# Causal convolution with per-position tap weights: where the tap weights of the fourth tap group are kept, and which engine multiplies with them

## The chip, the cores and the metric

The kernel runs on one core of a Trainium2 chip. The metric is the device time of one execution in microseconds; the time before is the median of three runs, 1239.92 us (1238.9 to 1240.16). The profile is that of one further execution.

The engines that are named here: PE is the matrix engine (TensorE), DVE the vector engine (VectorE), ACT the activation engine (ScalarE), POOL is GpSimd, and SP (SyncE) issues transfers. SBUF is the large on-chip memory, PSUM the small one into which PE writes. [...]

## The reference, cut to what matters

The network has four parts, each added to the residual: a causal convolution, a feed-forward layer with 4-bit rounding, a layer with a learned update, and a mixture of experts. The change lies in the first part alone:

```
avg  = cumsum(x, axis=1) / arange(1, l + 1)          # running mean, per channel
ci   = avg, split into H = 16 heads of d = 8 channels
pc   = ci @ W_pe + b_pe                              # 2 * 31 values per head and position
energy = stt + sigmoid(gate) * dyn                   # 31 energies
w    = softmax(energy, axis=-1)                      # 31 tap weights per head and position
out  = sum over k of w[:, :, k] * padded[:, k : k + l, :]   # for each of the 8 channels
v    = out @ W_fc.T + residual; then a layernorm
```

There are B = 8 sequences of L = 512 positions with 128 channels.

## The kernel before

`sequence_conv` works through the eight sequences. The 31 taps are cut into four groups g = 0 to 3 of eight taps, so that 16 heads x 8 taps fill the 128 partitions, and a row holds the 512 positions. For a sequence b and a group g:

- `gate` and `tap` (matmuls at L358, two banks of the pool `ps_e` in turn) give the two halves of `pc`. ACT turns the gate into a sigmoid in two steps (L366, L367). `energy` on DVE forms the energy `en` (L390) and the running maximum `top` (L394, L396).
- `turn_top` (PE, L401), `greatest` (DVE L406, then an ACT copy `mw`, L408) and `turn_greatest` (PE `mb`, L413) bring the largest energy of each head and position back to all partitions. `less` (DVE, L416) subtracts it from all four groups at once.
- `weigh` (ACT) takes the exponential twice: for groups 0 to 2 into a PSUM tile `w` (L427), each group with a bank of its own (tags w0, w1, w2 of the pool `ps_w`), and for all four groups into SBUF, in place (`en`, L429).
- `part_sums` and `sums` (PE `pn` L435, ACT copy `dn` L440, PE `sm` L445) add up the weights; `invert` (DVE L449, ACT L451) and `turn_inverse` (PE `rb` L456, ACT copy `rbs` L458) spread the inverse over the partitions. The tiles tt, mb, pn, sm and rb all use the single bank of the pool `ps_m`, so each waits until the one before it has been read. `mb` therefore waits for the copy `rbs`.
- The products of weights and shifted inputs. `base` holds, for the eight channels of a head, the shifted inputs; it comes by way of DRAM (`far` L349, eight loads L352, issued by SP). For groups 0 to 2 DVE multiplies six channels (`product`, L484, 128x3072, weights from PSUM), POOL two (`shared`, L473, two instructions of 128x512, weights from SBUF). For group 3 DVE multiplies all eight channels, with weights from SBUF (128x4096), in the sequences 0 to 5. In the sequences 6 and 7 `last_weights` (ACT, L463) copies the weights of group 3 into a bank of `ps_e`, and POOL takes two channels there too.
- `add_up` (PE `cv`, L493, 16 matmuls) sums a group's products over taps into one bank. The product tiles `pr` have three buffers in turn. `scale_down` (DVE, L500), `project` (PE, L505, L506), `norm1` (DVE statistics, then small POOL steps) and `finish` (ACT L524, POOL L528, L529) end a sequence; `means` (PE `av` L343, ACT copy `avg` L346) begins one.

The sequences are interleaved by hand: in the loop over b, `cur` is being multiplied while the energies of `nxt` and the gates of `then` are formed, and the end of `old` is worked off. On PE, DVE, ACT and in most of POOL's work the order of instructions is the order in which the program calls them: `Line` ties each instruction to the one before it on its engine. What an engine waits for, everything behind it on that engine waits for too.

In the loop the part that matters reads, before the change, in this order: `product(cur, 1)`, `greatest(nxt)`, `turn_inverse(cur)`, `taps(then, 0)`, `turn_greatest(nxt)`, `add_beta(b)`, `add_up(cur, 1)`, `norm1(old)`, `scaled(b + 4)`, then (sequences 6 and 7 only) `last_weights` and `shared` of group 3, `product(cur, 2)`, `add_up(cur, 2)`, and towards the end `less(nxt)`, `weigh(nxt, 0, 1)`, `means(b + 3)`, `weigh(nxt, 1, 4)`, `product(cur, 3)`, `add_up(cur, 3)`. Sequence 0 is written out ahead of the loop in much the same order.

Of the kernel before, what the change touches and what calls it, by code (L numbers as in the profile page):

```python
# [8 lines left out]
F32 = mybir.dt.float32  # L9
# [5 lines left out]
PSUM = bass.MemoryType.PSUM  # L15
DRAM = bass.MemoryType.DRAM

P = 128
B, L, D = 8, 512, 128
# [111 lines left out]
def flat(ap):  # L131
    return ap.rearrange("p a b -> p (a b)")
# [17 lines left out]
def sequence_conv(cx):  # L150
# [11 lines left out]
    nc, tc, ins = cx.nc, cx.tc, cx.ins  # L162
    KK, NGR = 8, 4
    NJ, ND = 4, 2
    NV, NP = 6, 3
# [6 lines left out]
    with ExitStack() as st:  # L172
# [4 lines left out]
        ps_e = st.enter_context(tc.tile_pool(name="a_pse", bufs=2, space=PSUM))  # L177
        ps_m = st.enter_context(tc.tile_pool(name="a_psm", bufs=1, space=PSUM))
        ps_c = st.enter_context(tc.tile_pool(name="a_psc", bufs=1, space=PSUM))
        ps_p = st.enter_context(tc.tile_pool(name="a_psp", bufs=1, space=PSUM))  # L180
        ps_w = st.enter_context(tc.tile_pool(name="a_psw", bufs=1, space=PSUM))
        vec, ten, act, gp = cx.vec, cx.ten, cx.act, cx.gp


# [83 lines left out]
        def stats0(lo, hi):  # L268
            for b in range(lo, hi):
                stats(grp(cx.x, b), mv0[:, b * G : (b + 1) * G, :])  # L270
# [90 lines left out]
        def gate(s, g, place=(ps_e, "e")):  # L361

            e = spread(s, 1, g, "eg", place)
            sg = p2.tile([P, L], F32, tag="sg", name="sg", bufs=4)
            s.setdefault("sg", {})[g] = sg
            act(nc.scalar.activation(sg, e, AF.Tanh, bias=half[:, g : g + 1], scale=0.5))  # L366
            act(nc.scalar.activation(sg, sg, AF.Copy, bias=0.5, scale=0.5))  # L367

        def tap(s, g):

            s.setdefault("ev", {})[g] = spread(s, 0, g, "ev")
# [5 lines left out]
        def taps(s, half_):  # L377
            for g in (2 * half_, 2 * half_ + 1):
                tap(s, g)
# [5 lines left out]
        def energy(s, g):  # L385
            if g == 0:
                s["en"] = p2.tile([P, NGR, L], F32, tag="en", name="en", bufs=3)
                s["top"] = p2.tile([P, L], F32, tag="top", name="top")
            en, top = s["en"], s["top"]
            vec(nc.vector.scalar_tensor_tensor(  # L390
                en[:, g, :], s["ev"][g], bias[:, 0, g : g + 1], s["sg"][g], ALU.add, ALU.mult
            ))
            if g == 0:
                vec(nc.vector.tensor_scalar(top, en[:, 0, :], bias[:, 2, 0:1], None, ALU.add))  # L394
            else:
                vec(nc.vector.scalar_tensor_tensor(top, en[:, g, :], bias[:, 2, g : g + 1], top, ALU.add, ALU.max))  # L396
# [6 lines left out]
        def greatest(s):  # L403

            mx = p2.tile([P, G, H], F32, tag="mx", name="mx")
            vec(nc.vector.tensor_reduce(mx, s["tt"].rearrange("p j (h k) -> p j h k", h=H), AX.X, ALU.max))  # L406
            s["mw"] = mw = p2.tile([P, G, H, KK], F32, tag="wide", name="mw")
            act(nc.scalar.copy(mw, mx.unsqueeze(3).to_broadcast([P, G, H, KK])))  # L408
# [12 lines left out]
        def weigh(s, lo, hi):  # L421

            en = s["en"]
            for g in range(lo, hi):
                if g < NP:
                    w = ps_w.tile([P, L], F32, tag=f"w{g}", name="w")
                    act(nc.scalar.activation(w, en[:, g, :], AF.Exp, bias=bias[:, 2, g : g + 1]))  # L427
                    s["w"].append(w)
                act(nc.scalar.activation(en[:, g, :], en[:, g, :], AF.Exp, bias=bias[:, 2, g : g + 1]))  # L429
# [12 lines left out]
        def sums(s):  # L442
            s["sm"] = sm = ps_m.tile([P, G, H], F32, tag="m", name="sm")
            for j in range(G):
                ten(nc.tensor.matmul(sm[:, j, :], s["dn"][:, j * P : (j + 1) * P], fold, start=True, stop=True))  # L445
# [7 lines left out]
        def turn_inverse(s):  # L453
            rb = ps_m.tile([P, G, P], F32, tag="m", name="rb")
            for j in range(G):
                ten(nc.tensor.transpose(rb[:, j, :], s["rw"][:, j].rearrange("p a b -> p (a b)"), cx.ident))  # L456
            s["rbs"] = rbs = p2.tile([P, L], F32, tag="rbs", name="rbs")
            act(nc.scalar.copy(rbs, flat(rb)))  # L458

        def last_weights(s):  # L460

            w = ps_e.tile([P, L], F32, tag="e", name="w")
            act(nc.scalar.copy(w, s["en"][:, NP, :]))  # L463
            s["w"].append(w)

        def shared(s, lo=0, hi=NP):

            s.setdefault("pr", [])
            for g in range(lo, hi):
                pr = p2.tile([P, DH, L], F32, tag="pr", name="pr", bufs=3)  # L470
                for d in range(NV, DH):
                    at = slice(KK * g, KK * g + L)
                    gp(nc.gpsimd.tensor_tensor(pr[:, d, :], s["base"][:, d, at], s["en"][:, g, :], ALU.mult))  # L473
                s["pr"].append(pr)

        def product(s, g, lo=0, hi=DH):

            if g == len(s["pr"]):
                s["pr"].append(p2.tile([P, DH, L], F32, tag="pr", name="pr", bufs=3))
            in_psum = g < len(s["w"])  # L480
            hi = min(hi, NV if in_psum else DH)
            w = s["w"][g].unsqueeze(1) if in_psum else s["en"][:, g : g + 1, :]
            at = slice(KK * g, KK * g + L)
            vec(nc.vector.tensor_tensor(  # L484
                s["pr"][g][:, lo:hi, :], s["base"][:, lo:hi, at], w.to_broadcast([P, hi - lo, L]), ALU.mult
            ))
# [11 lines left out]
        def scale_down(s):  # L498
            s["cs"] = cs = p2.tile([P, L], F32, tag="cs", name="cs", bufs=1)
            vec(nc.vector.tensor_tensor(cs, s["cv"], s["rbs"], ALU.mult))  # L500
# [39 lines left out]
        vec(nc.vector.tensor_scalar(half, bias[:, 1, :], 0.5, None, ALU.mult))  # L540
        stats0(3, 5)
        cur = seq[0]
        for g, place in enumerate(((ps_w, "w0"), (ps_w, "w1"), (ps_w, "w2"), (ps_c, "c"))):
            gate(cur, g, place)
            tap(cur, g)
            energy(cur, g)
# [33 lines left out]
        gates(then, 0)  # L580
        stats0(5, B)
        greatest(nxt)
        turn_inverse(cur)
        taps(then, 0)
        turn_greatest(nxt)
# [18 lines left out]
        for b in range(1, B):  # L604
            cur, nxt, then, old = seq[b], seq.get(b + 1), seq.get(b + 2), seq.get(b - 1)
            shared(cur)
            product(cur, 0)
            if b > 1:
                finish(seq[b - 2], nc.gpsimd)
            part_sums(cur)  # L610
            sums(cur)
            if old:
                scale_down(old)
                project(old)
            add_up(cur, 0)
            if nxt:
                for g in (2, 3):
                    energy(nxt, g)
            invert(cur)
            if nxt:  # L620
                turn_top(nxt)
            if then:
                gates(then, 0)
            product(cur, 1)
            if nxt:
                greatest(nxt)
            turn_inverse(cur)
            if then:
                taps(then, 0)
            if nxt:  # L630
                turn_greatest(nxt)
            add_beta(b)
            add_up(cur, 1)
            if old:
                norm1(old, nc.gpsimd)
            if b + 4 < B:
                scaled(b + 4)
            if b == B - 3:
                ffn.load(flat(tri)[:, : ffn.NW], cur["spread"])
            if b >= B - 2:  # L640
                last_weights(cur)
                shared(cur, NP, NGR)
            product(cur, 2)
            add_up(cur, 2)
            if then:
                for g in (0, 1):
                    energy(then, g)
                gates(then, 1)
                taps(then, 1)
            if nxt:  # L650
                less(nxt)
                weigh(nxt, 0, 1)
            if b + 3 < B:
                seq[b + 3] = means(b + 3)
            if nxt:
                weigh(nxt, 1, NGR)
            if b < B - 1:
                product(cur, 3)
                add_up(cur, 3)
# [9 lines left out]
        q = Fp4.of(cx, ffn.raw, ffn.NW, inv[:, :nb], inv[:, P : P + nb], parts, quot)  # L669
# [7 lines left out]
        q.scales()  # L677
        q.divide()
        act(nc.scalar.activation(warm, cx.eps[1e-5], AF.Silu))
        q.addends([ps_w.tile([P, L], F32, tag=f"w{i}", name="up")[:, : hi - lo] for i, (lo, hi) in enumerate(q.parts)])  # L680
        pj, v = cur["pj"], p2.tile([P, G, D], F32, tag="v", name="v")
        mv = p2.tile([P, G, 2], F32, tag="mv", name="mv")
        for _ in norm.stats(1):
# [21 lines left out]
        place = p2.tile([P, L], F32, tag="sg", name="quot", bufs=4)  # L705
# [1369 lines left out]
```

## Time and profile before

| what | value |
|---|---|
| median of three runs | 1239.92 us |
| the profiled execution | 1229.96 us |
| its span, first to last instruction | 1228.1 us |
| granted TensorE clock, mean | 0.976 |
| busy share of the span: PE, DVE, ACT, POOL | 91%, 62%, 41%, 60% |
| PE weight loads, beside the matmuls | 56% |
| start of `sm` (L445) of the sequences 1 to 7 | 73.03, 99.41, 125.75, 152.09, 178.43, 202.79, 224.49 us |

The shares of the whole span mix parts that have different limits. The convolution takes about the first 240 us. Since each sequence has its `sm` matmuls once, the distances between their starts are the time per sequence: 26.38, 26.34, 26.34, 26.34, 24.36 and 21.70 us.

A timeline row gives start, duration, engine, line, operation, output and inputs with their shapes; in brackets stands how long the engine was idle before it, and what ended that. A row of the chain of waits gives start, duration, engine and tile.

### The profile page before, as it was taken

The numbers are of one execution on the slowest core, as the hardware profiler recorded it, in microseconds if no ns is written. First come the engines' busy times: TensorE is split into PE (matmuls) and PEld (weight loads), VectorE is DVE, ScalarE is ACT, GpSimd is POOL, SyncE is SP. The second block draws the span as 40 slices with busy tenths as digits, with TensorE's granted clock in tenths as the row PEclk, the third lists the DMA queues.
The fourth block names the chain that finished last, engine by engine and source line by source line (L and its number), as shares of the span: only waits on it lengthen the run. The fifth ranks groups of instructions, "written<-read, shape, count | busy, mean of one in ns | idle before, by whom it ended". The sixth has DMA issues, their size and how long they took to land.

```text
span 1228.1 us, 15912 instructions
## 1 busy us (share of the span) xinstructions
PE 1112.0 (91%) x5475; PEld 682.0 (56%) x5475; DVE 761.9 (62%) x1801; ACT 498.8 (41%) x1050; POOL 736.0 (60%) x728
## 2 busy tenths in 40 slices
PE   7999998767987999999988999999999997999993
PEld 4333343345666555555566555555476666878773
DVE  6899999989996544444455444444466887123364
ACT  4655544445667322222244222223343444243331
POOL 1356666745644888888822888888500666355563
PEclk8999999989999999999999999999999998999997
DMA  5223444951000000000000000000000111221256
GB/s 157 90 82 94 120 117 141 383 150 49 1 1 1 1 1 1 1 1 1 0 1 1 1 1 1 1 0 1 1 1 3 43 44 43 63 70 53 67 199 208
DMA packets 54607, 67.29 MB, mean 55 GB/s; under 512 B 6927, under 2 KB 32350, under 8 KB 54528
## 3 DMA queue, kind: packets, MB, share of 16 engines
q1 hardware_dynamic: 48544, 56.57, 15.2%
q0 software_dynamic: 4608, 8.43, 2.1%
q10 hardware_dynamic: 1376, 1.29, 0.3%
q8 instruction: 43, 0.70, 0.2%
q14 instruction: 36, 0.29, 0.1%
HBM read 40.00 MB, written 27.13 MB: 55 GB/s over the span
## 4 chain that ended last, share of the span: by engine, by line
PE 63%; DVE 19%; ACT 9%; issue 4%; POOL 2%; DMA 2%; ACTq 0%; DVEq 0%; POOLq 0%
PE ph L1614 5%; PE sum L1589 5%; PE pp L1604 5%; PE sum L1588 4%; PE po L1998 4%; PE sum L1590 4%; PE pb L1566 4%; PE pa L1564 4%; PE ph L1985 4%; DVE v L859 3%; PE cv L493 2%; DVE pr L484 2%; PE pt L1597 2%; PE o L1354 2%; PE gu L974 2%
## 5 line engine op out<-in xcount | busy, mean ns | idle before, releaser
L1577 POOL TENSOR_TENSOR ds<-sw,s 128x512 f32<-128x512 f32 x64 | 81.2, 1268 | 74.9 <-DVE sw L1572 74.9
L1579 POOL TENSOR_TENSOR ds<-ds,s 128x512 f32<-128x512 f32 x64 | 110.4, 1725 | 5.0
L1570 ACT COPY b<-pb 128x512 f32<-128x512 f32 x64 | 37.5, 586 | 169.6 <-PE pb L1566 164.6
L1811 POOL DMA_INDIRECT rows<-xr,slot x64 | 62.6, 978 | 66.2 <-PE ph L1338 30.9
L1988 ACT ACTIVATE ht<-ph,b 128x512 f32<-128x512 f32 (+2 forms) x104 | 57.0, 576 | 107.3 <-PE ph L1985 105.9
L473 POOL TENSOR_TENSOR pr<-base,en 128x512 f32<-128x512 f32 x52 | 75.0, 1472 | 38.0 <-ACT en L429 37.3
L2012 POOL DMA_INDIRECT res<-ye,xe x60 | 58.5, 974 | 64.4 <-DVE ye L2010 28.0
L1574 DVE TENSOR_TENSOR h<-sw,b 128x512 f32<-128x512 f32 x64 | 50.0, 781 | 75.6 <-ACT b L1570 75.5
L484 DVE TENSOR_TENSOR pr<-base,w 128x3072 f32<-128x3072 f32 (+2 forms) x27 | 86.3, 3206 | 0.8 <-ACT w L427 0.8
L1578 POOL TENSOR_TENSOR ds<-sw,ds 128x512 f32<-128x512 f32 x64 | 82.8, 1294 | 5.0
L1580 POOL TENSOR_TENSOR ds<-ds,b 128x512 f32<-128x512 f32 x64 | 81.9, 1280 | 5.0
L1604 PEld LDWEIGHTS pp<-proj,ht 128*128 128x128 f32 x512 | 67.1, 191 | 30.8 <-issue 29.7
L1599 ACT COPY ht<-pt 128x512 f32<-128x512 f32 x64 | 37.6, 587 | 103.0 <-PE pt L1597 103.0
L1998 PE MATMUL po<-w,ht 128*128 128x128 f32 (+1 forms) x640 | 77.1, 277 | 0.0
L1985 PE MATMUL ph<-xt,w 128*128 128x512 f32 (+2 forms) x208 | 72.3, 492 | 3.9 <-DVE xt L1968 3.9
L1572 DVE TENSOR_TENSOR sw<-pa,s 128x512 f32<-128x512 f32 x64 | 44.3, 692 | 49.4 <-ACT s L1568 49.4
L1998 PEld LDWEIGHTS po<-w,ht 128*128 128x128 f32 (+1 forms) x640 | 73.9, 188 | 0.6
L1616 DVE TENSOR_TENSOR db<-ph,sw 128x512 f32<-128x512 f32 x64 | 44.3, 692 | 45.3 <-PE ph L1614 45.3
L1614 PE MATMUL ph<-proj_t,dpt 128*128 128x512 f32 x128 | 71.6, 641 | 0.0
L493 PE MATMUL cv<-pr,sel 128*32 128x512 f32 x512 | 61.4, 605 | 8.9 <-DVE pr L484 8.8
L1564 PE MATMUL pa<-gate,kt 128*128 128x512 f32 x128 | 66.0, 598 | 3.0 <-ACT qt L1197 0.9
L1604 PE MATMUL pp<-proj,ht 128*128 128x128 f32 x512 | 67.5, 275 | 0.0
(366 smaller groups left out, 2604.5 us busy)
## 6 DMA issues: line engine op xcount, KB each, us to landing
base<-far SPq DMA_DIRECT2D x64, 268.0 KB, 5.5
rows<-empty SPq DMA_DIRECT2D x1, 5005.0 KB
res<-zero SPq DMA_DIRECT2D x1, 4096.0 KB, 26.8
own<-zero SPq DMA_DIRECT2D x2, 2048.0 KB, 18.8
w<-in_L_ffn_W SPq DMA_DIRECT2D x16, 256.0 KB, 5.0
y<-res SPq DMA_DIRECT2D x16, 256.0 KB, 5.3
xe<-rows SPq DMA_DIRECT2D x7, 585.0 KB, 4.3
y<-own SPq DMA_DIRECT2D x12, 256.0 KB, 4.7
```

The costliest lines, as they stand in the source:

```text
L473: gp(nc.gpsimd.tensor_tensor(pr[:, d, :], s["base"][:, d, at], s["en"][:, g, :], ALU.mult))
L484: vec(nc.vector.tensor_tensor(s["pr"][g][:, lo:hi, :], s["base"][:, lo:hi, at], w.to_broadcast([P, hi - lo, L]), ALU.mult))
L493: ten(nc.tensor.matmul(s["cv"][32 * j : 32 * (j + 1), :], sel[:, i].rearrange("p a h -> p (a h)"), s["pr"][g][:, i * NJ + j, :], start=(g ...
L1564: nc.tensor.matmul(pa, ki, gate, start=True, stop=True)
L1577: nc.gpsimd.tensor_tensor(ds, sw, s, ALU.mult)
L1578: nc.gpsimd.tensor_tensor(ds, sw, ds, ALU.subtract)
L1579: nc.gpsimd.tensor_tensor(ds, ds, s, ALU.add)
L1580: last = nc.gpsimd.tensor_tensor(ds, ds, b, ALU.mult)
L1604: nc.tensor.matmul(pp, ht[:, c * P : (c + 1) * P], proj[:, c, :], start=(c == 0), stop=(c == NF - 1))
L1614: nc.tensor.matmul(ph, dpt, proj_t, start=True, stop=True)
L1985: ten(nc.tensor.matmul(ph[:, :n], self.w1[:, e, c * P : (c + 1) * P], xt[:, :n], start=True, stop=True))
L1998: ten(nc.tensor.matmul(po[:m, i - lo, :], ht[:, c, (i - lo) * P : (i - lo) * P + m], self.w2[:, e, c, :], start=(c == 0), stop=(c == NF - ...
```

## The change

The pool `ps_w` has one tag with three banks that are taken in turn, where each group had a bank of its own. The weights of group 3 are copied into one of these banks (`last_weights`) in every sequence, and POOL multiplies two channels of group 3 in every sequence, DVE the other six. `last_weights` now stands between `greatest(nxt)` and `turn_inverse(cur)`. Each sequence takes four tiles from three banks: the tile of group 2 of the next sequence gets the bank in which the group 3 weights of this sequence were.

```diff
-        ps_w = st.enter_context(tc.tile_pool(name="a_psw", bufs=1, space=PSUM))
+        ps_w = st.enter_context(tc.tile_pool(name="a_psw", bufs=3, space=PSUM))
...
                 if g < NP:
-                    w = ps_w.tile([P, L], F32, tag=f"w{g}", name="w")
+                    w = ps_w.tile([P, L], F32, tag="w", name="w")
                     act(nc.scalar.activation(w, en[:, g, :], AF.Exp, bias=bias[:, 2, g : g + 1]))
...
         def last_weights(s):
 
-            w = ps_e.tile([P, L], F32, tag="e", name="w")
+            w = ps_w.tile([P, L], F32, tag="w", name="w")
             act(nc.scalar.copy(w, s["en"][:, NP, :]))
             s["w"].append(w)
...
-        for g, place in enumerate(((ps_w, "w0"), (ps_w, "w1"), (ps_w, "w2"), (ps_c, "c"))):
+        for g, place in enumerate(((ps_w, "w"), (ps_w, "w"), (ps_w, "w"), (ps_c, "c"))):
...
         greatest(nxt)
+        last_weights(cur)
+        shared(cur, NP, NGR)
         turn_inverse(cur)
...
             if nxt:
                 greatest(nxt)
+            last_weights(cur)
             turn_inverse(cur)
...
-            if b >= B - 2:
-                last_weights(cur)
-                shared(cur, NP, NGR)
+            shared(cur, NP, NGR)
             product(cur, 2)
...
-        q.addends([ps_w.tile([P, L], F32, tag=f"w{i}", name="up")[:, : hi - lo] for i, (lo, hi) in enumerate(q.parts)])
+        q.addends([ps_w.tile([P, L], F32, tag="w", name="up")[:, : hi - lo] for i, (lo, hi) in enumerate(q.parts)])
```

## The prediction

> **What bounds the kernel now.** The change lies in the first 240 us, so I read that stretch alone. First the busy time of each engine in one sequence, from one `sm` to the next (columns: PE, PE weight loads, DVE, ACT, POOL, then clock, DMA share, GB/s):
>
> ```profile
> core 0: us, PE busy (x) PEld busy (x) DVE busy (x) ACT busy (x) POOL busy (x), PEclk, DMA share, GB/s
> 125.75:152.09 26.34, 24.59 (x133) 10.49 (x133) 25.49 (x25) 15.20 (x28) 16.03 (x27) 1.00 0.33 94
> ```
>
> DVE is busiest (25.49 of 26.34 us), but PE is only 0.9 us behind it. Shares can't say which of the two sets the 26.34. So next the waits of both engines in three such sequences (99.41 to 178.43 us; total, times, longest):
>
> ```profile
> PE sm L445 <- ACT dn L440: 3.3, 4, 0.8
> PE mb L413 <- ACT rbs L458: 1.6, 3, 0.5
> PE pn L435 <- ACT en L429: 0.9, 3, 0.3
> ...
> DVE mx L406 <- PE tt L401: 1.7, 3, 0.6
> DVE rs L449 <- PE sm L445: 0.3, 2, 0.2
> ```
>
> DVE waits for PE, twice a sequence; PE waits for ACT and never for DVE. So PE and ACT turn in a ring, each waiting for the other, and DVE follows it. The chain of waits says the same:
>
> ```profile
> 125.75 1.07 PE sm L445 x8
> ...
> 133.99 0.63 ACT sg L367
> 134.62 0.51 ACT mw L408
> 135.67 0.66 PE mb L413 x4
> 136.32 3.57 PE cv L493 x32
> 139.89 1.07 PE eg L358 x2
> ...
> 144.09 2.17 PE av L343 x8
> 146.29 0.59 ACT avg L346
> ...
> 152.09 1.06 PE sm L445 x8
> ```
>
> It goes from PE to ACT at the gates (132.03), back to PE at `mb`, to ACT at the second gates and at `avg`, back to PE at `sm`, and round again after exactly 26.34 us. No DVE row is in it from 99.41 to 183.23. The timeline of ACT shows the place that matters:
>
> ```profile
> 134.53 0.60 ACT L408 COPY mw<-mx 128x512 f32<-128x512 f32 x1
> 135.03 0.58 ACT L458 COPY rbs<-rb 128x512 f32<-128x512 f32 x1
> 135.51 1.65 ACT L301 ACTIVATE xn<-x,off,rs 128x128 f32<-128x128 f32 x4
> ```
>
> ACT works without a gap from 132.03 to `rbs`, which ends at 135.61; `mb` starts on PE at 135.67, after an idle 0.53 us that the PE timeline puts down to `rbs`. Whatever is put ahead of `rbs` on ACT is on the ring.
>
> Where the ring is not the bound, at the first and the sixth sequence, PE waits for the very product that the change makes shorter:
>
> ```profile
> 68.61 1.92 PE L493 MATMUL cv<-pr,sel 128*32 128x512 f32 x16 [1.33 <-DVE pr L484]
> ...
> 198.07 1.92 PE L493 MATMUL cv<-pr,sel 128*32 128x512 f32 x16 [1.30 <-DVE pr L484]
> ```
>
> **Removed on DVE.** Six products of 128x4096 become 128x3072. Neighbours in the DVE timeline: the large one starts at 140.92, the next (3072, weights in PSUM) at 145.26, the one after at 148.52. So 4.34 against 3.26 us: 1.08 us each, 6.5 us in all. In the ring sequences (1 to 4) none of it shows: DVE only waits longer for PE.
>
> **Added on POOL.** Twelve 128x512 products. Such pairs took 2.53 to 2.75 us, so 2.7 a sequence. POOL comes free at 131.65 (`add_beta`), then waits 1.38 for the statistics; the pair would end at about 134.4 and push the 18 small steps of `norm1` from ending at 138.01 to about 140.8. Behind them: ACT's `v` (L524, 150.07), 9 us cover, and POOL's next products, which wait for `en` until 145.0, 4 us cover. The pair needs the buffer that `cv` of group 0 read until 130.54: no wait. `cv` of group 3 needs the pair at 146.18. So 0; without cover up to 2.7 a sequence.
>
> [...]
>
> **Added on ACT, the term that decides.** Six copies `w` of 128x512 from SBUF to PSUM. In the sequences 6 and 7 the same copy (L463, 210.69 and 230.40) took 0.60 and 0.59. What it takes of ACT's queue is the distance to the next start: between like copies 0.50 (`mw` to `rbs`) and 0.48 (`rbs` to `xn`). Bounds: 0.48, and the full 0.60. I take 0.50, the row at the same place. It stands right ahead of `rbs`, so `rbs`, `mb` and everything after move by 0.50 in each sequence.
>
> - Sequence 0: `mb` 56.71 to 57.21. Down PE: `av` ends at 67.79 for 67.29, the shorter product ends at about 67.4 for 68.56, so `cv` starts at 67.8 for 68.61. But `pn` also needs ACT's exponentials, behind `avg`, which follows `av`: the third ended at 70.60 and will at 71.1; in the steady sequences `pn` ends 1.72 after it (149.55 to 151.27), so at 72.8, where it ended at 72.36. The 0.8 that DVE gives is lost, and `sm` comes 0.46 late.
> - Sequences 1 to 4: 0.50 each on the ring, 2.00.
> - Sequence 5: no `means` is left, the chain before passes to DVE (from 183.85 to 222.4 without a gap). `sm` of 6 is 0.50 later still (2.96), but DVE has gained 1.08 and loses about 0.6, since product 0 of sequence 6 now waits for its weights from ACT (`w` at 196.16, which moves to 199.1). `tt` of the last sequence then ends at 208.19 + 2.96 = 211.15 and DVE's `mx` starts there, for 208.73 before: 2.42. DVE's own path would have it at about 210.9. So this sequence adds nothing (2.46 to 2.42).
> - Sequences 6 and 7 had the copy already, behind `rbs`. Now it delays `mb` at 210.85 by about 0.3; `less` follows product 2, which ends at 213.71, 2.2 after `mb`: covered. In 7 ACT is idle 3.11 us before `rbs`: covered.
>
> **Banks in turn.** The `w` of group 2 waits until DVE has read the group 3 weights of the sequence before. Behind it on ACT: two more `en`, `v`, `dn`, that is the ring. DVE's product ends near 144.2, `w` comes at 148.13 + 0.5: 4 us cover. In the last sequence it is `w` at 218.63 against a product end at 219.19, 0.6 late; the last `en` ends at 221.2 for 220.7, and `pn` starts at 221.82 after its own wait for `cv`. So 0; with the cover gone a microsecond late is one on the ring. The two `ps_e` banks that this frees in 6 and 7 save nothing: no gates are left to wait for them.
>
> **SP.** The eight loads of `base` for sequence 2 now stand ahead of `far` of sequence 3 (6.23 us of issue at 68.64). That `far` is next needed at 94.69, 19 us later. The weight `w_down` of the next layer moves behind loads too; its tile is first read at 236.92, 60 us on. So 0, and a late `base` would cost its lateness.
>
> **Sum.** 0.46 + 2.00 - 0.04 = +2.4 us on the profiled execution: 1229.96 to 1232.4. The timed runs are 10 us longer than it (1239.92), and no page says where. If PE is the slower part there, the ring also binds in sequence 5, and its 0.50 counts: +2.9. I take the middle, +2.7: 1242.6. With 0.60 a copy and six of them: +3.6, 1243.5. Own range of this case: 1241.8 to 1243.6. After the convolution all is in series with it, and moves as a whole.
>
> **The rivals.**
> - DVE is the bound after all (for: 25.49 of 26.34 busy; in the second sequence 26.20 of 26.38; against: it waits for PE, PE never for it). Then 6 x 1.08 = 6.5 us come out: 1233.4. This is the other side; it decides if DVE is later than PE at `cv` of group 3, where it was 0.84 us early (145.34 against 146.18). Chance 0.10.
> - The copy costs nothing, because ACT finds room ahead of `rbs` (against: no gap from 132.03 on). Then only the end counts: DVE would be 1.08 early at `mx`, of which `tt` leaves 208.73 - 208.19 = 0.5. So 1239.4. Chance 0.13.
> - The turn of the banks or POOL's added work gets onto the ring. POOL's lock also lengthens DVE's `top` (L396 1.46 beside POOL, 0.75 alone). If `w` of group 2 is held 1 us in six sequences: 1242.6 + 6 = 1248.6. Against: 4 us cover. Chance 0.09.
> - That the change doesn't do what it says is ruled out by its instruction order: all eight sequences have the 128x3072 product, the POOL pair and the copy ahead of `rbs`.
>
> **How the numbers follow.** The forecast has 0.68. Runs of this kernel can tell about 0.2% from no change, 2.5 us, so the line lies at 1242.4, inside the forecast's own range. Of 0.68, 0.43 lie above it and 0.25 below; with the bank rival slower is 0.52. Same is 0.25 and the free copy's 0.11: 0.36. Faster is the DVE rival and the rest of the free copy: 0.12. The range takes in the free copy at nearly its full price and reaches past six copies of 0.60 towards the bank rival: 1239.0 to 1245.0.
>
> **What would show it.** Right: the distance from `sm` to `sm` is 26.84 for 26.34; PE's idle time before `mb` is 1.0 for 0.53; on ACT the row L463 stands between L408 and L458; DVE waits for PE about 1 us more a sequence, most of it ahead of `mx`, `cs` or the first product; the products of 128x4096 are gone; POOL's L473 has 64 rows. Wrong: a distance below 26.34, which says that DVE was the bound, or `w` of group 2 with an idle time ended by DVE.

## The result and the profile after

The kernel after the change takes 1244.2 us (median of 20 runs, 1241.87 to 1248.39), the kernel before 1240.41 us (20 runs beside them). The ratio is 1.0031, with an interval of 1.0021 to 1.0040: 3.8 us slower, between 2.6 and 5.0. The forecast was 1242.6 us, 2.7 us more than before.

The profiled executions can't be subtracted from each other: the one after has a span of 1240.2 us, 12.1 more than the 1228.1 before. Where these 12.1 us lie follows from the start times of the same instructions in the two traces:

| stretch | before, us | after, us | difference |
| --- | --- | --- | --- |
| start to `sm` of sequence 0 | 42.23 | 39.61 | -2.6 |
| `sm` of 0 to `sm` of 6 | 160.56 | 163.62 | +3.06 |
| `sm` of 6 to `sm` of 7 | 21.70 | 20.16 | -1.5 |
| on to the last pass of the learned layer (first `ph`, L1338 before, L1339 after) | 699.3 | 700.9 | +1.6 |
| that pass, to the first expert's `ph` (L1985 before, L1986 after) | 131.2 | 141.6 | +10.4 |
| the rest of the span | 173.1 | 174.3 | +1.2 |

Only the second row is shown by the experiments to be the change. A second profile of the kernel before (b_again) differs from the first by 2.5 us in the first row alone, the clock differs in the third (0.92 before, 1.00 after), and the 10.4 us come with the chip, as b_again shows (131.1 us in that pass on its chip, 142.3 in e1_copy_behind_rbs on another). In the steady sequences it is the same each time: from `sm` to `sm` the six distances were 30.80, 26.38, 26.34, 26.34, 26.34 and 24.36 us, and are 31.31, 26.89, 26.85, 26.85, 26.85 and 24.87. Every one is 0.51 longer. First the engines' busy times in one steady sequence after (columns as in the prediction):

```profile
124.66:151.51 26.85, 24.58 (x132) 10.50 (x133) 24.90 (x25) 15.70 (x29) 18.55 (x29) 1.00 0.33 96
```

DVE has lost 0.6 us of work (25.49 to 24.90) and POOL has gained 2.5 (16.03 to 18.55); PE does the same work as before (24.59 and 24.58), and the sequence is longer than it was. DVE's product alone became 1.08 shorter; part of that is gone again because `top` (L396) beside POOL's products took 1.74 us here where it took 1.46. ACT's timeline in the same sequence, and PE's `mb` after and then before:

```profile
133.44 0.60 ACT L408 COPY mw<-mx 128x512 f32<-128x512 f32 x1
133.95 0.58 ACT L463 COPY w<-en 128x512 f32<-128x512 f32 x1
134.47 0.58 ACT L458 COPY rbs<-rb 128x512 f32<-128x512 f32 x1
134.94 1.65 ACT L301 ACTIVATE xn<-x,off,rs 128x128 f32<-128x128 f32 x4
```

```profile
135.10 0.66 PE L413 MATMUL mb<-ident,mw 128*128 128x128 f32 x4 [1.05 <-ACT rbs L458]
```

```profile
135.67 0.66 PE L413 MATMUL mb<-ident,mw 128*128 128x128 f32 x4 [0.53 <-ACT rbs L458]
```

The new copy L463 stands between `mw` and `rbs`. From its start to the next one are 0.52 us, where its duration reads 0.58: like copies overlap by 0.06. `mb` starts 0.63 after `rbs` begins (0.64 before), and PE's idle time ahead of it has grown from 0.53 to 1.05. The waits of three such sequences (97.81 to 178.36 us; total, times, longest) answer to those of the prediction:

```profile
PE sm L445 <- ACT dn L440: 3.3, 4, 0.8
PE mb L413 <- ACT rbs L458: 3.1, 3, 1.0
PE pn L435 <- ACT en L429: 0.9, 3, 0.3
DVE cs L500 <- PE cv L493: 2.0, 3, 0.7
DVE mx L406 <- PE tt L401: 1.7, 3, 0.6
DVE pr L484 <- ACT w L427: 1.3, 3, 0.4
DVE rs L449 <- PE sm L445: 0.2, 1, 0.2
```

One wait has changed on PE, the one for `rbs` (1.6 to 3.1). PE still waits for nothing of DVE. DVE now waits in two new places, ahead of `cs` (0.7 each) and of the first product (0.4 each): together 1.1 a sequence, which is the 0.6 us of work that it lost and the 0.5 by which the sequence became longer. No DVE row stands in the chain of waits from 97.81 to 182 us. And the two places at which PE had waited 1.33 and 1.30 us for the long product are gone; the row of sequence 0 now has no idle time in front of it:

```profile
65.11 1.92 PE L493 MATMUL cv<-pr,sel 128*32 128x512 f32 x16
```

Even so sequence 0 became 0.51 longer: the start of `cv` isn't what its `sm` waits for. PE waits behind that `cv` for ACT's exponentials (0.29 us) and `dn` (0.68 us).

### The profile page after: what moved, and what is told of

It is laid out like the page before. It is cut to its first block, busy times and chain, and to the rows that moved or that the text cites. A ratio compares the mean times of both kernels' runs of the same rounds, so it can differ in the third digit from the quotient of the medians.

```text
span 1240.2 us, 15948 instructions
## 1 busy us (share of the span) xinstructions
PE 1109.6 (89%) x5475; PEld 678.0 (55%) x5475; DVE 759.1 (61%) x1801; ACT 502.3 (41%) x1056; POOL 747.1 (60%) x740
## 4 chain that ended last, share of the span: by engine, by line
PE 65%; DVE 17%; ACT 11%; issue 4%; DMA 2%; POOL 2%; ACTq 0%; DVEq 0%; POOLq 0%
PE ph L1615 5%; PE sum L1590 5%; PE pp L1605 5%; PE sum L1589 4%; PE sum L1591 4%; PE po L1999 4%; PE pb L1567 4%; PE pa L1565 4%; PE ph L1986 4%; PE cv L493 3%; DVE v L860 3%; PE pt L1598 2%; PE o L1355 2%; PE ph L1339 2%; ACT sg L366 2%
## 5 line engine op out<-in xcount | busy, mean ns | idle before, releaser
L473 POOL TENSOR_TENSOR pr<-base,en 128x512 f32<-128x512 f32 x64 | 85.9, 1371 | 40.8 <-ACT en L429 34.4
L484 DVE TENSOR_TENSOR pr<-base,w 128x3072 f32<-128x3072 f32 (+2 forms) x33 | 106.4, 3233 | 2.9 <-ACT w L427 2.9
L1986 PE MATMUL ph<-xt,w 128*128 128x512 f32 (+2 forms) x208 | 70.9, 484 | 4.0 <-DVE xt L1969 3.9
L1590 PE MATMUL sum<-db,k 128*128 128x512 f32 x128 | 66.1, 598 | 1.6 <-DVE db L1617 1.6
```

The lines of the kernel that those rows point to most:

```text
L484: vec(nc.vector.tensor_tensor(s["pr"][g][:, lo:hi, :], s["base"][:, lo:hi, at], w.to_broadcast([P, hi - lo, L]), ALU.mult))
L1590: nc.tensor.matmul(sums[1], ki, db, **kw)
L1986: ten(nc.tensor.matmul(ph[:, :n], self.w1[:, e, c * P : (c + 1) * P], xt[:, :n], start=True, stop=True))
```

## Experiments

All ratios are to the kernel before, run on the same chip beside the experiment, with 95% intervals.

The first four kernels, on one chip (before: 1241.3 us), take the change apart. The diffs are cut to the lines that matter: sequence 0, written out ahead of the loop, is edited in the same way. Theory: the place of the one ACT copy is the whole cost. Rivals: POOL's extra pairs, the turn of the three banks (each holds one 128x512 tile of the pool `ps_w`) or products of DVE and POOL that hold each other up cost something, or the shorter product gives something back.

**e1_copy_behind_rbs.** The changed kernel, with the copy behind `rbs`. POOL pairs, short products and banks in turn stay.

```diff
             if nxt:
                 greatest(nxt)
-            last_weights(cur)
             turn_inverse(cur)
...
             if b + 4 < B:
                 scaled(b + 4)
+            last_weights(cur)
```

> The changed kernel with one thing moved: ACT copies the group 3 weights behind rbs and the scaling, not ahead of rbs; POOL's pairs, DVE's smaller products and the banks in turn stay. Theory 'ring' (the copy ahead of rbs lengthens the PE-ACT ring, nothing else costs): sm to sm in the steady sequences back from 26.85 to 26.34 us, PE's idle time before mb back from 1.05 to 0.53, time 0 to 1 us below the kernel before (ratio 0.999 to 1.000). Rival 'POOL and banks' (POOL's added products, their lock against DVE, or the wait for a bank cost the time): sm to sm stays near 26.85 and the ratio near 1.003.

Measured 1241.31 us, 0.9999 [0.9990, 1.0008]. PE and ACT in the steady sequence:

```profile
135.76 0.66 PE L413 MATMUL mb<-ident,mw 128*128 128x128 f32 x4 [0.53 <-ACT rbs L458]
```

```profile
137.16 0.57 ACT L463 COPY w<-en 128x512 f32<-128x512 f32 x1
```

PE's wait is back at 0.53, `sm` to `sm` at 26.34. The copy is still made, in time that ACT had free: behind it ACT is idle for another 3.35 us until the next gates. Everything else in the change together costs nothing that can be seen, and gives nothing.

**e2_copy_alone.** The changed kernel, with the copy where it was put but without its use in sequences 0 to 5: DVE multiplies all eight channels of group 3 again, and POOL's pair is gone.

```diff
             last_weights(cur)
+            if b < B - 2:
+                cur["w"].pop()
             turn_inverse(cur)
...
-            shared(cur, NP, NGR)
+            if b >= B - 2:
+                shared(cur, NP, NGR)
```

> The changed kernel with the copy and the banks in turn, but in sequences 0 to 5 nobody uses the copied weights: DVE multiplies all eight channels of group 3 from SBUF as before, POOL takes none. Ring: sm to sm 26.85, idle before mb 1.05, ratio 1.003 to 1.004. POOL and banks, if POOL is the cost: sm to sm 26.34, ratio 1.000; if the banks are: sm to sm near 26.85, but with an idle time before the w of group 2 that DVE ends.

Measured 1244.62 us, 1.0028 [1.0018, 1.0037]. `sm` to `sm` is 26.85 and the wait ahead of `mb` 1.05, as with the whole change. So the copy costs the same whether DVE's product is shorter or not.

**e3_copy_twice.** The changed kernel, with the copy made twice.

```diff
             act(nc.scalar.copy(w, s["en"][:, NP, :]))
+            act(nc.scalar.copy(w, s["en"][:, NP, :]))
```

> The changed kernel with the copy done twice in a row in every sequence. Ring: sm to sm 27.35 (another 0.50), idle before mb 1.55, ratio 1.0055 (about 3 us more than the changed kernel). POOL and banks: sm to sm 26.85, ratio 1.003.

Measured 1248.53 us, 1.0056 [1.0042, 1.0069]. `sm` to `sm` is 27.48: 0.51 for the first copy, 0.63 for the second. The wait ahead of `mb` is now 1.67. ACT's timeline:

```profile
135.97 0.58 ACT L463 COPY w<-en 128x512 f32<-128x512 f32 x1
136.59 0.59 ACT L464 COPY w<-en 128x512 f32<-128x512 f32 x1
137.11 0.58 ACT L458 COPY rbs<-rb 128x512 f32<-128x512 f32 x1
```

The second copy starts 0.62 after the first, with no overlap, and not 0.52 as `rbs` does after it; both copies write the same tile, and whether that is the cause isn't shown. That is the 0.1 by which the distance missed the expected 27.35. From `sm` of 0 to `sm` of 6 this kernel took 167.39 us, 6.83 more than before, and its median is 7.2 more: what the copies add to the sequences is what the runs show.

**e4_no_copy.** The kernel before, with the POOL pair and the short product of group 3 in all sequences, and without the copy in 0 to 5: DVE takes the weights of group 3 from SBUF there.

```diff
-            hi = min(hi, NV if in_psum else DH)
+            hi = min(hi, NV)
...
             if b >= B - 2:
                 last_weights(cur)
-                shared(cur, NP, NGR)
+            shared(cur, NP, NGR)
```

> The kernel before, with POOL taking two channels of group 3 in every sequence and DVE six, but with the weights of group 3 read from SBUF in sequences 0 to 5: no copy there, no banks in turn. Ring: sm to sm 26.34, idle before mb 0.53, ratio 0.999 to 1.000. POOL and banks, if POOL is the cost: ratio 1.003 or more, since DVE's product with two SBUF inputs now runs beside more POOL work.

Measured 1242.32 us, 0.9998 [0.9988, 1.0009]; `sm` to `sm` 26.34, the wait ahead of `mb` 0.53. Here DVE is 0.7 us less busy than in the kernel before (24.81 us of the sequence), with nothing put on ACT, and the time doesn't move. DVE is not the bound, also where nothing hides that.

The next four, on another chip (before: 1229.3 us there), ask two things: where the 10 us of the last pass come from, and whether work taken off the PE-ACT ring makes the kernel faster, which it must if the ring is the bound.

**b_again.** The kernel before, unchanged, profiled once more.

> The kernel before, profiled once more. All five profiles of the other kernels have 141.5 to 142.2 us from the first ph matmul of the layer's last pass (L1338 of the kernel before) to the first expert matmul (L1985), the first profile of the kernel before 131.1. If that one was an execution in which this part went faster, and the 10 us between its 1229.96 and the timed 1239.92 lie there, this profile has about 142 there, a span near 1239, and 26.34 from sm to sm as before. If the kernels differ there, it has 131 again.

Measured 1227.09 us, a single run. Its last pass took 131.1 us (131.2 before). That does not mean that the kernels differ there: on this chip all have 129 to 131 (f1_mw_on_pool 129.4, f2_weights_late 129.5, f3_both 131.1), where on the chip of the first four all had about 142 (142.3 in e1_copy_behind_rbs). So the 10 us belong to the chip that a run falls on. What slows that pass there wasn't tried.

**f1_mw_on_pool.** e4_no_copy, with the copy `mw` on POOL in place of ACT in sequences 0 to 5: one copy fewer ahead of `rbs`.

```diff
-            act(nc.scalar.copy(mw, mx.unsqueeze(3).to_broadcast([P, G, H, KK])))
+            wide = mx.unsqueeze(3).to_broadcast([P, G, H, KK])
+            if pool:
+                gp(nc.gpsimd.tensor_copy(mw, wide))
+            else:
+                act(nc.scalar.copy(mw, wide))
```

> The run without the copy, with mw (the copy ahead of rbs, L408) taken from ACT to POOL in sequences 0 to 5: the opposite of the change, one copy less on the ring. Ring: sm to sm 25.84 for 26.34, ratio 0.9975 (3 us less). Rival 'DVE is right behind': with 24.4 us of work DVE still has room at 25.84, so it should not stop at more than that; if it does, DVE's idle time is gone. Rival 'POOL is late': the idle time before mb is ended by POOL and stays 0.5 or grows, ratio 1.000 or more.

Measured 1226.9 us, 0.9974 [0.9963, 0.9986]. `sm` to `sm` 25.88, 0.46 less; `mb` has no idle time ahead of it, as PE's waits in three sequences show (97.68 to 175.31 us):

```profile
PE sm L449 <- ACT dn L444: 2.5, 3, 0.8
PE pn L439 <- ACT en L433: 0.9, 3, 0.3
```

The ring was the bound in this direction too.

**f2_weights_late.** e4_no_copy, with the PSUM weights of groups 1 and 2 copied from the finished exponentials, so that ACT makes the exponentials that `pn` on PE waits for one after the other, with the copies behind them.

```diff
-                if g < NP:
+                if g == 0:
...
+        def late_weights(s, g):
+            w = ps_w.tile([P, L], F32, tag=f"w{g}", name="w")
+            act(nc.scalar.copy(w, s["en"][:, g, :]))
+            s["w"].append(w)
...
+            late_weights(cur, 1)
             part_sums(cur)
+            late_weights(cur, 2)
             sums(cur)
```

> The run without the copy, with the other leg of the ring shortened: the PSUM weights of groups 1 and 2 are copied from the finished exponentials, one ahead of dn and one behind it, in place of a second exponential ahead of en. Then pn waits less for en. Ring: en of group 3 is done at 148.7 for 150.2 on the clock of the first profile, pn is bound by PE and ends near 150.7, dn starts there for 151.45: sm to sm 25.6 to 25.7, ratio 0.996 to 0.997. If only the leg through rbs counts: 26.34, ratio 1.000.

Measured 1227.66 us, 0.9986 [0.9976, 0.9996]. The distances are of two kinds: 25.42, less than expected, with a granted clock of 1.00, and 27.02 with a clock of 0.94.

**f3_both.** f2_weights_late with f1's `mw` on POOL.

```diff
-                greatest(nxt)
+                greatest(nxt, then is not None)
```

> Both: mw on POOL and the late weights. Ring: sm to sm 25.1, ratio 0.994 (7 us less), and DVE's idle time nearly gone. Rival 'DVE is right behind': DVE stops it between 25.1 and 25.6, with its idle time at 0; ratio 0.995 to 0.997.

Measured 1225.31 us, 0.9973 [0.9962, 0.9983]: no better than f1 alone. Three sequences, and the 3.4 us after the start of the last of them (columns as before; the clock is the third figure from the end):

```profile
92.96:119.51 26.55, 24.98 (x133) 11.55 (x133) 25.40 (x26) 14.30 (x28) 23.58 (x33) 0.94 0.37 104
119.51:144.46 24.95, 23.39 (x133) 10.42 (x133) 24.36 (x25) 14.29 (x28) 22.53 (x30) 1.00 0.38 103
144.46:170.99 26.53, 24.97 (x133) 11.78 (x133) 24.28 (x25) 12.75 (x24) 22.44 (x30) 0.94 0.32 86
145.60:149.00 3.40, 3.40 (x20) 3.14 (x23) 3.40 (x3) 0.62 (x1) 3.32 (x3) 0.52 0.82 226
```

Every second sequence is 1.6 us longer, which is what the 3.40 us at a clock of 0.52 come to (3.40 x 0.48 = 1.6), and the ring's gain of 1.4 us (26.34 to 24.95) is lost there. The stretch begins about 1.2 us behind PE's longest wait, 1.34 us for `dn` ahead of `sm`. That made a theory for the last two, on a third chip (before: 1241.29 us): a shorter wait there keeps the clock up.

**g1_dn_early.** f3_both, with `part_sums` (and its copy `dn`) behind both late copies and ahead of `finish`, so that PE's wait is split and shorter.

```diff
-            if b > 1:
-                finish(seq[b - 2], nc.gpsimd)
             late_weights(cur, 1)
-            part_sums(cur)
             late_weights(cur, 2)
+            part_sums(cur)
             sums(cur)
+            if b > 1:
+                finish(seq[b - 2], nc.gpsimd)
```

> The run with both, with ACT's dn ahead of v (both PSUM copies, then dn, then v): PE then waits about 0.65 us before sm for 1.34. In the run with both, PE's clock fell to 0.94 in two of three steady sequences, right behind that 1.34 us gap, and these took 26.5 for 24.95 us. If the gap brings the clock down, the clock stays at 1.00 here, sm to sm is 24.6 to 25.0 in all steady sequences, and the ratio 0.992 to 0.994. If the clock falls for another reason, distances still alternate between 25 and 26.5, ratio near 0.997. Rival 'DVE is right behind': with 24.3 us of work it ends the gain at about 24.8, with no idle time left.

Measured 1234.56 us, 0.9949 [0.9935, 0.9963], 6.7 us less than before: the fastest of all against its own base, and faster than both kernels of this case. But not for the reason given:

```profile
92.08:118.48 26.40, 25.17 (x132) 11.51 (x132) 25.41 (x25) 14.41 (x28) 23.58 (x33) 0.94 0.38 106
118.48:143.27 24.79, 23.57 (x132) 10.49 (x132) 24.37 (x25) 14.40 (x28) 22.54 (x30) 1.00 0.35 100
```

The slow sequences are still there, though PE now waits 0.67 us ahead of `sm` and 0.34 ahead of `pj`. The theory of the long wait falls; what brings the clock down stays open. From `sm` of 0 to `sm` of 6 it took 154.70 us, 5.9 less than before, and so most of its gain is in the sequences.

**g2_dn_early_psum.** The same edits on e1_copy_behind_rbs, that is with the change's weights in PSUM and its three banks.

> The same on the changed kernel with its copy behind rbs and the scaling: group 3 weights in PSUM, three banks in turn. DVE's group 3 product has one SBUF input, so it should not hold up POOL's small steps (one of them took 3.38 us for 0.20 beside that product in the run with both). Ring: ACT has one more copy, in a gap of 3.9 us, so sm to sm as in the run beside it, within 0.1, and the ratio within 0.001 of it. If the turn of three banks costs (w of group 2 waits for the group 3 product, ahead of dn), an idle time before that copy that DVE ends, and 0.3 us or more a sequence.

Measured 1238.64 us, 0.9983 [0.9971, 0.9995], 4 us behind g1. A miss in the ratio, which should have been within 0.001 of g1's: the distances from the `sm` of 2 on to that of 6 equal g1's within 0.01 us, and no wait ahead of the copied `w` shows there. In the two profiles, whose spans differ by 3.1 us, 1.8 lie ahead of the first `sm` and 1.3 between the `sm` of 0 and of 7, 0.9 of it in the last of these steps. Why it is slower wasn't settled.

## Why the prediction was right, step by step

- **What bounds the kernel.** Right, and shown from both sides: a copy more on the ring ahead of `rbs` costs 0.51 a sequence (e2_copy_alone), two cost 1.14 (e3_copy_twice), one fewer gives 0.46 (f1_mw_on_pool), and less work on DVE gives nothing (e4_no_copy). With it falls the rival that DVE is the bound. The free copy falls too: it is free behind `rbs` on the same engine (e1_copy_behind_rbs), and not ahead of it.
- **The price of a copy.** Taken as 0.50 from the distance between starts, measured 0.51. The duration that the trace shows, 0.58 to 0.60, would have made it 3.6 us over six.
- **Removed on DVE, added on POOL.** Taken as 0 each, and e1_copy_behind_rbs, which has both and the turn of the banks, is at 0.9999. POOL's own products became shorter: the first pair of the steady sequence took 2.54 us for 2.75, and the six products of the second sequence 8.42 (2.54 + 5.88) for 10.72. In the profile before, the six POOL products that started while a 128x4096 product of DVE (weights from SBUF) still ran took 1.48 to 3.64 us and ended 1.14 to 1.17 us after it; the pair at 210.04, beside a DVE product with weights from PSUM, took 2.54, about 1.27 each. PE waited for none of POOL's products, before or after.
- **The turn of the banks.** Also taken as 0, and right in the steady sequences. In the last one the foreseen wait came (0.48 us for 0.6; an idle time of `w` that DVE ends, which the prediction names as a sign of being wrong), and in the profile after it was not covered. ACT's rows there:

```profile
219.42 0.69 ACT L427 ACTIVATE w<-en,bias 128x512 f32<-128x512 f32 x1 [0.48 <-DVE pr L484]
...
222.75 0.59 ACT L440 COPY dn<-pn 128x512 f32<-128x512 f32 x1
```

  From this wait to `dn` ACT has no idle time, so `dn`, and PE's `sm` behind it, are late by most of it: from the last `mx` to `sm` are 14.46 us, where e4_no_copy, without the wait and with the same clock of 1.00, has 14.06. In the profile before PE was later than ACT there (`dn` waited 1.79 us for `pn`), because 16 matmuls of `cv` took 2.83 us where 1.92 is usual, at a lower clock (0.92 from the `sm` of 6 to that of 7); e1_copy_behind_rbs and e2_copy_alone, also at 0.92, have the 0.48 and cover it. The step compared the end of the last `en` with the start of `pn` on that slower PE, and left out `v` (1.49 us), which ACT does ahead of `dn`. So this 0 was 0.4 at full clock.
- **Sequence 0.** +0.46 predicted, +0.51 measured, for the reason given: `cv` starts without a wait, but `pn` hangs on ACT.
- **Sequence 5 and the way to the last one.** Here too a term was mis-sized. The step said that DVE, with 1.08 us gained and 0.6 lost, would have its own path to `mx` of the last sequence ready before `tt`, which would set it: 2.42 us late. Counted from the first `sm`, `mx` came at 208.73 - 42.23 = 166.50 before and at 208.93 - 39.61 = 169.32 after: 2.82 late, without a wait, so DVE's own path decided. The rows of DVE's timeline after, and then before, show how it came there:

```profile
193.55 3.34 DVE L484 TENSOR_TENSOR pr<-base,w 128x3072 f32<-128x3072 f32 x1
197.31 3.35 DVE L484 TENSOR_TENSOR pr<-base,w 128x3072 f32<-128x3072 f32 x1 [0.41 <-ACT w L427]
...
201.96 1.70 DVE L396 SCALAR_TENSOR_TENSOR top<-en,bias,top 128x512 f32<-128x512 f32 x1
...
208.93 0.67 DVE L406 TENSOR_REDUCE mx<-tt 128x64 f32<-128x512 f32 x1
```

```profile
202.58 0.86 DVE L396 SCALAR_TENSOR_TENSOR top<-en,bias,top 128x512 f32<-128x512 f32 x1
...
208.73 0.67 DVE L406 TENSOR_REDUCE mx<-tt 128x64 f32<-128x512 f32 x1
```

  The first row, the shortened product, starts 2.57 us late against `sm` (153.94 for 151.37), the next one 1.99: as foreseen, 1.08 gained and about half of it lost in the wait for ACT's `w` (0.41). Then `top` takes 1.70 for 0.86 and puts 0.83 back on. POOL's products run beside it in both kernels; after the change `top` starts 0.1 us behind the start of one of them (201.84), before it 1.0 behind (201.62), and in both it ends 0.55 us after the end of that product. The two traces hold 48 rows of L396: the 22 with no such POOL product beside them take 0.75 or 0.76 us, and the 26 others, of 0.85 to 1.81, all end 0.54 to 0.56 us after the end of one. So by these rows `top` waits for POOL's product to end, and a shift of DVE against POOL sets how long. Without this, DVE's path would have been 1.99 us late, near the 2.2 that the prediction gave it (210.9). e1_copy_behind_rbs has the same (1.69): its `mx` comes at 166.27, not 1.08 but 0.23 earlier than before. The prediction had this lengthening of `top` (1.46 for 0.75) in the rival of the banks only, as POOL's lock, and not on DVE's path in the one place where DVE decides.
- **The sum.** +2.7 was taken: +2.4 from the rows, raised by 0.3 for a reason that was wrong (next point). That 2.7 lies nearer to the runs than 2.4 is luck; what 2.4 lacks are the 0.4 at the last `mx` (2.82 for 2.42) and the 0.4 of the banks, together +3.2. The runs say +3.8 [2.6, 5.0], an interval that holds 2.7 and 3.2; its middle lies just above the +1.9 to +3.7 that the prediction's own case allowed. Between the `sm` of 6 and of 7 profiles can be compared only at the same clock: it was 0.92 in both profiles of the kernel before and in three of the first four experiments, and 1.00 in the kernel after and in e4_no_copy. From the `sm` of 0 to that of 7 the kernel after is 3.4 us longer than e4_no_copy, and e2_copy_alone 2.7 to 3.2 longer than the kernel before, b_again and e1_copy_behind_rbs. The rest of the 3.8 isn't settled and lies within its interval.
- **The 10 us between profile and runs.** The reason offered, that PE is the slower part in the timed runs and the ring would bind in sequence 5 too, was wrong. The 10 us lie in the last pass and come with the chip; of sequence 5 they say nothing.

## What to carry to other kernels

In this loop two engines that wait for each other in turn, PE and ACT, set the pace, and DVE was busier than PE (25.49 us of 26.34 for 24.59) without counting: look for the engine that nobody waits for, and don't spend anything to relieve it. A small instruction costs by what is queued behind it: the same copies cost some 3 us ahead of `rbs` and nothing behind it. For its price on a queue take the distance between starts (0.52 us here) and not the duration (0.58); and where an engine's row is longer beside another's, as `top` was with 1.70 us for 0.86, it is so on the path too: a saving that shifts it in time may be spent there.

## What the runs showed of the hardware

- The shorter loops met a lower clock. The steady sequences had a clock of 1.00 in the kernel after (`sm` to `sm` 26.85), in the kernel before and e4_no_copy (26.34) and in f1_mw_on_pool (25.88). In the four kernels that reach 24.8 to 25.5, every second sequence or so had a clock of 0.94 and took 1.6 us more (f2_weights_late 27.02 for 25.42, f3_both 26.55 for 24.95, g1_dn_early 26.40 for 24.79, g2_dn_early_psum 26.39 for 24.80); in f3_both 3.40 us of such a sequence had a clock of 0.52. The length of PE's waits doesn't sort these kernels: in f3_both the longest in the sequence ahead was 1.35 us, and in g1_dn_early 0.67, while f1_mw_on_pool kept its clock with waits of up to 0.82. What brings the clock down in these kernels stays open.
- The kernel before took 1229.3 us on one chip and 1241.3 on two others, most of the difference being in one pass, which took 129 to 131 us in the profiles on the first and 141 to 142 in those on the others (142.3 in e1_copy_behind_rbs, 141.7 in g1_dn_early).
- A small POOL instruction was held for a whole DVE product. In f3_both, POOL's timeline and then DVE's:

```profile
134.71 3.38 POOL L147 TENSOR_TENSOR rs<-rs,sq 128x4 f32<-128x4 f32 x1
```

```profile
134.68 3.35 DVE L493 TENSOR_TENSOR pr<-base,en 128x3072 f32<-128x3072 f32 x1
```

  Its usual time is 0.20 us. In g2_dn_early_psum, where DVE takes these weights from PSUM, the longest of this line was 0.50.
